# A graph and expert kernel: POOL in the layer norms between two layers, one product for nodes and scores, transposed counts copied by ACT, buffers for the scatters' rows

## The chip, the cores and the metric

The kernel runs on one core of one Trainium2 chip. A core has five engines that work side by side, each through its own list of instructions, in order: TensorE (PE, matrix products, with weight loads PEld beside them), VectorE (DVE), ScalarE (ACT), GpSimd (POOL) and SyncE (SP, which here only starts transfers). Transfers (DMA) are started by SP, ACT or POOL. An instruction that needs another engine's result waits on a semaphore at the head of its engine's list, and all behind it waits too. The metric is the time of one execution in microseconds (us), the median over runs.

## The reference

Four layers on 3125 nodes of 256 features with 50000 edges, each with a residual:

```python
x = x + gnn(layernorm(x))                 # L0_gnn: three graph convolutions
x = x + experts(layernorm(x))             # L0_ffn: 16 experts, best 2, layer norm behind
x = x + attention(layernorm(x))           # L1_gnn: graph attention, 4 heads, 64 wide
x = x + experts(layernorm(x))             # L1_ffn: 8 experts, best 2

def L0_ffn(x):                            # x: [nodes, 256]
    logits = x @ gate_w + gate_b
    top_w  = softmax(top2(logits))
    y = x + sum_k top_w[k] * expert[top_idx[k]](x)      # relu(x @ w1 + b1) @ w2 + b2
    return (y - mean(y)) / sqrt(var(y) + 1e-5) * gamma + beta

def L1_gnn(h):
    x  = h @ W                            # 256 -> 64
    el = x @ Wl.T ; er = x @ Wr.T         # scores, 4 heads each
    ...                                   # softmax over edges, weighted sums, elu
```

A graph convolution sums over edges, which the kernel does as a product with a dense matrix of edge counts between nodes.

## The kernel before

The nodes are padded to 3200, 25 tiles of 128 rows, in seven blocks (`BLK`): four of 512 nodes (4 tiles) and three of 384 (3 tiles). The stages follow each other:

1. 0 to 55 us: edges are loaded and turned into keys (L1194 to L1290).
2. 55 to 295: the counts (L1314 to L1365). For each window of destinations DVE makes one-hot rows `os` (L1323) and `od` (L1326), PE multiplies them into `pc` (L1328), ACT copies the sums to `cr` (L1331). For each of the 25 tiles PE transposes `cr` in four groups (1024, 1024, 1024 and 128 columns, L1337) into `pt`, a copy brings each group to `ct`, PE sums `ct` (`op`, L1344), and SP stores it in DRAM as `cntT`. The copies are ACT's (L1342), but from tile 8 on that of the first group is DVE's (L1340). `pt` and `ct` have two buffers each.
3. 295 to 855: three graph convolutions (L1411 to L1452). A block's sums `agg` (L1431) go to `aT` (the first half copied by DVE, L1434), through the product `gout` (L1440) and `gy` (DVE, L1443) to X. In the third layer each finished block goes on to the norm and to `R0.route` (`Router.steps`, L787 to L910), which picks two experts for each token. For each token it makes a row `meta` of 8 numbers (L858 to L872) and two places `at_i0`, `at_i1` (L903), and POOL scatters the rows to DRAM (`slots`, L905), one indirect DMA for each tile and choice. `meta` and `at_i` come from the pool `gp`, with two buffers. The steps of a block's routing are spread among PE's products for the next blocks.
4. 855 to 883: the last block's routing and the plan of the experts.
5. 883 to 1144: the first expert layer (`experts`, L968 to L1142): ACT copies `cT` (L1090), loads of `w1t` and `slot`, gathers `xs` (L1017, POOL), products (L1038, L1048), results scattered to `res` (L1065, POOL).
6. 1144 to 1237: the end of that layer (L1499 to L1565), the stage that changes most, below.
7. 1237 to 1772: attention (L1572 to L1722), with the second routing inside it, 1772 to 1800 its end and plan.
8. 1800 to 2093: the second expert layer and the output.

Stage 6 runs for each block: for each tile `results` (L1144) loads the two results of each token as `r` (SP, ten buffers), PE adds `r[:,0]`, `r[:,1]` and the base as three products with the identity (L1150, `rsum`), ACT copies the sum to HB (L1151). Then DVE takes the moments (`moments`: L692, L693 and L695, square root by ACT L675, a Newton step by DVE L680 to L685), makes z = (HB - mean) * gamma (L1515) and X += z * rstd (L1517), and the moments of X for the attention's layer norm, with `nm` = -mean * rstd (L1521). ACT makes h (L1525), PE transposes it (L1528), ACT copies `hT` (L1529), PE makes `px`, the projection with nodes along the columns (L1532), ACT copies it to `xT` (L1533). For each tile PE makes the scores `pe` from `xT` (L1536) and, from `hT` once more, the projection with nodes along the rows, `py` (L1539), which ACT copies to `xn` (`spare`, L1541). At the end DVE copies all scores from `pe` to `lr` (L1542), and the first step of the attention takes their maximum (L1545). A scheduler orders every engine's list by priorities; where a pool has no free buffer for a tile, its first instruction waits for the readers of the last one.

Of the kernel before, what the change touches and what calls it, by code (L numbers as in the profile page):

```python
# [8 lines left out]
F32 = mybir.dt.float32  # L9
BF16 = mybir.dt.bfloat16  # L10
F16 = mybir.dt.float16
I32 = mybir.dt.int32
F32R = mybir.dt.float32r
AF = mybir.ActivationFunctionType
OP = mybir.AluOpType
# [4 lines left out]
P = 128  # L20
# [574 lines left out]
def fast(  # L595
# [35 lines left out]
    nc = tc.nc  # L631
    N, D = x.shape
    (NE,) = src.shape
    NT = -(-N // P)
    NP = NT * P
    REAL = N // NT
    DC = D // P
# [15 lines left out]
    small = ctx.enter_context(tc.tile_pool(name="small", bufs=2))  # L653
# [7 lines left out]
    ident = consts.tile([P, P], F32, name="ident")  # L661
# [76 lines left out]
    class Router:  # L738
# [48 lines left out]
        def steps(self, H, t0, U, work, psum, h0=None, pe=lambda i: i, kept=None):  # L787

            h0 = t0 if h0 is None else h0
            E, nm = self.E, self.name  # L790

            def wt(name, shape, dt=F32):
                return work.tile(shape, dt, name=f"{name}_{nm}", tag=f"{name}_{nm}")
# [6 lines left out]
            for n in kept or [4] * (U // 4) + [U % 4] * (U % 4 > 0):  # L800
                hb = work.tile([P, DC, 4 * P], F32, name=f"hb_{nm}", tag=f"hb_{nm}", bufs=1)
                for u in range(n):
                    pt = psum([P, DC, P])
# [48 lines left out]
                                                   op0=OP.mult, op1=OP.add)  # L852
                    cur = rest
            yield
            meta = wt("meta", [P, U, 8])
            if not kept:
                self.keep(H[:, h0:h0 + U, :], t0, U)
            nc.vector.tensor_copy(meta[:, :, 0], tok2[:, t0:t0 + U])  # L858
# [35 lines left out]
            for i in range(2):  # L894
                at = wt(f"at{i}", [P, U])
                nc.vector.tensor_tensor(hots[i], hots[i], row, op=OP.mult)
                nc.vector.tensor_reduce(at, hots[i], axis=AX.X, op=OP.add)
                off = wt(f"off{i}", [P, U])
                nc.vector.tensor_scalar(off, drop[:, t0:t0 + U], float((E * NT + 1) * P + i * PADS), unreal,
                                        op0=OP.add, op1=OP.mult)  # L900
                nc.vector.scalar_tensor_tensor(at, at, real, off, op0=OP.mult, op1=OP.add)
                at_i = wt(f"at_i{i}", [P, U], I32)
                nc.vector.tensor_copy(at_i, at)  # L903
                for u in range(U):
                    d = nc.gpsimd.indirect_dma_start(  # L905
                        out=self.slots, out_offset=bass.IndirectOffsetOnAxis(ap=at_i[:, u:u + 1], axis=0),
                        in_=meta[:, u, :], in_offset=None)
                    for e in self.sent:
                        tc.declare_no_dep(d.ins, e.ins, reason="every token has slots of its own")
                    self.sent.append(d)  # L910
# [230 lines left out]
            with tc.If(rest < E * NT):  # L1141
                tiles(most, TT)  # L1142

        def results(self, base, t, pool, psum):  # L1144

            r = pool.tile([P, 2, D], F32, name="r", bufs=10)
            nc.sync.dma_start(r, self.res[2 * P * t:2 * P * (t + 1), :].rearrange("(p k) d -> p k d", k=2))
            p = psum([P, D])
            for k, v in enumerate((r[:, 0, :], r[:, 1, :], base[:, t, :])):
                nc.tensor.matmul(p, ident, v, start=(k == 0), stop=(k == 2))  # L1150
            nc.scalar.copy(base[:, t, :], p)  # L1151


# [16 lines left out]
    with tc.tile_pool(name="edges", bufs=1) as ed, tc.tile_pool(name="ework", bufs=2) as ew:  # L1170
# [134 lines left out]
        with tc.tile_pool(name="ps_cnt0", bufs=2, space=PSUM) as ps_cnt0, \  # L1305
# [6 lines left out]
            for b, (s0, bw) in enumerate(BLK):  # L1312
                cr = ew.tile([P, NT, bw], F16, name="cr", tag="cr")
                nc.gpsimd.memset(cr.rearrange("p t (u q) -> p t u q", q=P)[:, :, :, REAL:], 0.0)  # L1314
                for dt in range(s0 // P, (s0 + bw) // P):
                    o = dt * P - s0
                    while wins and wins[0][0] < (dt + 1) * REAL:
                        i, w, c = wins.pop(0)
                        pc = ps_cnt0.tile([P, 512], F32, name="pc")
                        for k in range(c):  # L1320
                            if j % OS == 0:
                                os_ = ew.tile([P, P, OS], F16, name="os", bufs=3)
                                nc.vector.tensor_tensor(os_, ramps, by[0][:, None, j:j + OS].to_broadcast([P, P, OS]),  # L1323
                                                        op=OP.is_equal)
                            od = ew.tile([P, 512], F16, name="od", bufs=6)
                            nc.vector.tensor_scalar(od[:, :w * NT], ramp[:, :w * NT], by[1][:, j:j + 1], None,  # L1326
                                                    op0=OP.is_equal)
                            nc.tensor.matmul(pc[:, :w * NT], os_[:, :, j % OS], od[:, :w * NT], start=(k == 0), stop=(k == c - 1))  # L1328
                            j += 1
                        u = o + i - dt * REAL  # L1330
                        nc.scalar.copy(cr[:, :, u:u + w], pc[:, :w * NT].rearrange("p (d t) -> p t d", t=NT))  # L1331
                    ct = ew.tile([P, NP], F16, name="ct")
                    for q0 in range(0, NP, 1024):
                        w2 = min(1024, NP - q0)
                        pt = ps_tr.tile([P, 1024], F16, name="pt")
                        for q in range(w2 // P):
                            nc.tensor.transpose(pt[:, q * P:(q + 1) * P], cr[:, q0 // P + q, o:o + P], ident16)  # L1337

                        if dt >= 8 and q0 == 0:
                            nc.vector.tensor_copy(ct[:, q0:q0 + w2], pt[:, :w2])  # L1340
                        else:
                            nc.scalar.copy(ct[:, q0:q0 + w2], pt[:, :w2])  # L1342
                    for b2, (q0, w2) in enumerate(BLK):
                        nc.tensor.matmul(op[b2 // 4][32 * (b2 % 4):32 * (b2 % 4) + 32, :w2], ones16,  # L1344
                                         ct[:, q0:q0 + w2], start=(dt == 0), stop=(dt == NT - 1))
                        nc.sync.dma_start(cntT[b2][:, dt, :], ct[:, q0:q0 + w2])
                    if dt == 1:
                        R0.clear(HB[:, 9 * R1.Q:])
                        R1.clear(HB[:, :9 * R1.Q])
                    if dt == 8:  # L1350
                        mv, r = moments(X)
                nc.sync.dma_start(cnt[b], cr)
                ip = ps_in.tile([P, 512], F32, name="ip")
                for t in range(NT):
                    q = 32 * (t % 4)
                    nc.tensor.matmul(ip[q:q + 32, :bw], ones16, cr[:, t, :], start=(t < 4), stop=(t >= NT - 4))
                nc.scalar.copy(ins[:, s0:s0 + bw], ip[:, :bw])
                for t in range(s0 // P, (s0 + bw) // P):
                    nc.tensor.matmul(dg[:, 1, t:t + 1], ins[:, t * P:(t + 1) * P], c32, start=True, stop=True)
# [112 lines left out]
    xT = g1.tile([OD, NP], F32, name="xT")  # L1472
    spare = g1.tile([P, NH, 512], F32, name="spare")
    xn = spare.rearrange("p h n -> p (h n)")[:, :NT * OD].rearrange("p (t o) -> p t o", o=OD)
    lr = g1.tile([P, NT, 2, NH], F32, name="lr")
    fa = g1.tile([P, NT, NH], F32, name="fa")
    pj = g1.tile([P, NT, NH], F32, name="pj")
    wj = g1.tile([P, NT, NH], F32, name="wj")
# [3 lines left out]
    with tc.tile_pool(name="moe0", bufs=1) as mp:  # L1482
# [16 lines left out]
        with tc.tile_pool(name="ps_pre", bufs=2, space=PSUM) as ps, tc.tile_pool(name="tail", bufs=1) as mp:  # L1499
# [4 lines left out]
            nc.tensor.transpose(pw, wlr, ident[:2 * NH, :2 * NH])  # L1504
            nc.vector.tensor_copy(wlrT, pw)
            nc.vector.tensor_copy(wlb, wlrT[:, 0:NH, None].to_broadcast([OD, NH, P]))
            pe = ps.tile([P, NT, 2 * NH], F32, name="pe", bufs=1)
            for s0, w in BLK:
                t0, n = s0 // P, w // P
                for t in range(t0, t0 + n):  # L1510
                    R0.results(HBn, t, mp, rsum)
                mv, r = moments(HBn, t0, n)
                for i in range(n):
                    z = mp.tile([P, D], F32, name="z", bufs=2)
                    nc.vector.scalar_tensor_tensor(z, HBn[:, t0 + i, :], mv[:, i, 0:1], gamma,  # L1515
                                                   op0=OP.subtract, op1=OP.mult)
                    nc.vector.scalar_tensor_tensor(X[:, t0 + i, :], z, r[:, i:i + 1], X[:, t0 + i, :],  # L1517
                                                   op0=OP.mult, op1=OP.add)
                mv, r = moments(X, t0, n)
                nm = small.tile([P, n], F32, name="nm", tag="nm")  # L1520
                nc.vector.scalar_tensor_tensor(nm, mv[:, :, 0], -1.0, r, op0=OP.mult, op1=OP.mult)  # L1521
# [9 lines left out]
                for f in range(DC):  # L1531
                    nc.tensor.matmul(px[:, :w], wg[:, f, :], hT[:, f, :w], start=(f == 0), stop=(f == DC - 1))  # L1532
                nc.scalar.copy(xT[:, s0:s0 + w], px[:, :w])  # L1533
                for i in range(n):
                    t = t0 + i
                    nc.tensor.matmul(pe[:, t, :], xT[:, t * P:(t + 1) * P], wlrT, start=True, stop=True)  # L1536
                    py = ps.tile([P, OD], F32, name="py", tag="py")
                    for f in range(DC):
                        nc.tensor.matmul(py, hT[:, f, i * P:(i + 1) * P], wg[:, f, :],  # L1539
                                         start=(f == 0), stop=(f == DC - 1))  # L1540
                    nc.scalar.copy(xn[:, t, :], py)  # L1541
            nc.vector.tensor_copy(lr.rearrange("p t s h -> p t (s h)"), pe)  # L1542
            a_, b_ = lr[:, :, 0, :], lr[:, :, 1, :]
            top = small.tile([P, NH], F32, name="top")
            nc.vector.tensor_reduce(top, a_.rearrange("p t h -> p h t"), axis=AX.X, op=OP.max)  # L1545
# [228 lines left out]
```

## Time and profile before

Three runs took 2101.62, 2096.23 and 2097.72 us, the median is 2097.72. The profiled execution took 2094.98 us, with a span of 2093.2 us and a mean granted TensorE clock of 0.956. By stage (us busy):

| stretch | length | PE | DVE | ACT | POOL | clock |
|---|---|---|---|---|---|---|
| 0 to 55 edges | 55 | 8.0 | 39.6 | 2.1 | 25.0 | 1.00 |
| 55 to 295 counts | 240 | 213.3 | 210.1 | 159.6 | 6.5 | 1.00 |
| 295 to 660 convolutions 1, 2 | 365 | 355.4 | 88.2 | 215.2 | 0.0 | 0.98 |
| 660 to 883 convolution 3, routing | 223 | 185.4 | 105.0 | 92.5 | 54.2 | 0.90 |
| 883 to 1144 experts 1 | 261 | 250.9 | 99.5 | 71.4 | 113.2 | 0.96 |
| 1144 to 1237 end of experts 1 | 93 | 79.3 | 57.4 | 43.6 | 0.1 | 0.89 |
| 1237 to 1800 attention | 563 | 532.1 | 495.2 | 129.5 | 64.7 | 0.95 |
| 1800 to 2093 experts 2 | 293 | 269.0 | 93.2 | 77.8 | 105.5 | 0.94 |

An engine that is busy for most of a stretch may set its length; where none is, the stretch is a chain of waits between them, and the waits of that stretch have to be read.

### The profile page before, as it was taken

Reading aid. Unit: us, or ns where it says so; the run is one execution under the profiler, and the core shown is the slowest. Engines: PE = TensorE matmul, PEld = TensorE weight load, DVE = VectorE, ACT = ScalarE, POOL = GpSimd, SP = SyncE. Lnnn points to the kernel's source line nnn. Section 1 sums busy time; section 2 is a strip of 40 time slices with the busy share of each in tenths; the row PEclk is TensorE's granted clock in tenths of the full one; section 3 lists DMA queues with packets and bytes.
Section 4 is the critical chain, followed back from the end, with each engine's and each line's share of the span. In section 5 each row is a group of like instructions: output and inputs, shape, how many; then the busy total and the mean of one; then the engine's idle time right before and its main releaser. Section 6 shows DMA issues by size and latency. Waiting matters only on the chain. (4 is left out here: it accounts for less than half of the span.)

```text
span 2093.2 us, 31963 instructions
## 1 busy us (share of the span) xinstructions
PE 1893.4 (90%) x10944; PEld 1252.0 (60%) x10944; DVE 1188.1 (57%) x3825; ACT 791.7 (38%) x1611; POOL 369.1 (18%) x414
## 2 busy tenths in 40 slices
PE   1898979999999898699998988999999998699997
PEld 1444548898898677588887741222223232588886
DVE  7998863131124344443332768899998998434330
ACT  0367766565555534222222561212212222222221
POOL 4000000000000312254443000000300402344430
PEclk9999989999999999789999989999999999599998
DMA  5145664344344333665664601111011110465656
GB/s 148 53 176 217 227 220 133 110 129 129 116 115 147 112 91 94 198 201 168 182 192 139 213 1 51 39 48 61 28 54 43 43 39 28 122 182 164 193 160 197
DMA packets 172299, 259.91 MB, mean 124 GB/s; under 512 B 33476, under 2 KB 116658, under 8 KB 171100
## 3 DMA queue, kind: packets, MB, share of 16 engines
q1 hardware_dynamic: 148446, 211.87, 32.6%
q0 software_dynamic: 16016, 37.00, 5.6%
q10 hardware_dynamic: 7662, 8.84, 1.3%
q8 instruction: 93, 1.52, 0.3%
q14 instruction: 82, 0.67, 0.1%
HBM read 187.38 MB, written 70.27 MB: 123 GB/s over the span
## 5 line engine op out<-in xcount | busy, mean ns | idle before, releaser
L1431 PE MATMUL agg<-ar,parts 128*128 128x512 f32 (+1 forms) x2100 | 447.8, 371 | 7.6 <-ACT parts L1419 7.6
L1431 PEld LDWEIGHTS agg<-ar,parts 128*128 128x128 f32 x2100 | 383.6, 189 | 55.0 <-ACT parts L1419 7.7
L1702 DVE SCALAR_TENSOR_TENSOR HB<-ub,wj,cload 128x512 f32<-128x512 f32 (+1 forms) x420 | 268.6, 689 | 21.2 <-ACT ub L1606 9.9
L1426 ACT CAST ar<-cload 128x2560 fp32r<-128x2560 f16 (+1 forms) x105 | 220.8, 2103 | 147.1 <-PE agg L1431 133.5
L1038 PE MATMUL ph<-xsT,w1t 128*128 128x128 f32 x1792 | 239.2, 285 | 12.2 <-DVE xsT L1028 11.1
L1042 ACT ACTIVATE hid<-ph,b1s 128x128 f32<-128x128 f32 x448 | 128.1, 369 | 322.0 <-PE ph L1038 310.1
L1038 PEld LDWEIGHTS ph<-xsT,w1t 128*128 128x128 f32 x1792 | 220.4, 196 | 47.0 <-DVE xsT L1028 30.5
L1048 PE MATMUL py<-w2all,hid 128*128 x896 | 211.9, 380 | 0.0
L1590 PE MATMUL att<-HB,xp 128*64 128x512 f32 (+1 forms) x840 | 187.5, 567 | 0.0
L1048 PEld LDWEIGHTS py<-w2all,hid 128*128 128x128 f32 x896 | 162.1, 191 | 17.5
L1326 DVE TENSOR_SCALAR od<-ramp,by 128x450 f16<-128x450 f16 (+11 forms) x588 | 152.3, 320 | 22.1 <-PE pc L1328 21.0
L1434 DVE COPY aT<-agg 128x512 f32<-128x512 f32 (+1 forms) x21 | 13.3, 633 | 248.5 <-PE agg L1431 248.5
L1328 PE MATMUL pc<-od,os 128*128 128x450 f16 (+11 forms) x588 | 136.6, 334 | 17.6 <-DVE od L1326 9.5
L1059 DVE TENSOR_TENSOR to_i<-to,two 128x1 int32<-128x1 f32 x112 | 17.7, 158 | 237.4 <-DMA res_m<-y,to_i 237.4
L1065 POOL DMA_INDIRECT res_m<-y,to_i x112 | 110.4, 986 | 232.6 <-DVE y L1064 228.3
L905 POOL DMA_INDIRECT slots_m<-meta_m,at_i_m x100 | 107.8, 1078 | 209.0 <-DVE at_i_m L903 122.2
L1331 ACT CAST cr<-pc 128x400 f16<-128x400 f32 (+10 forms) x202 | 95.5, 503 | 63.8 <-PE pc L1328 48.9
L1017 POOL DMA_INDIRECT xs<-feats_m,slot x112 | 108.3, 967 | 61.7 <-issue 23.8
L1590 PEld LDWEIGHTS att<-HB,xp 128*64 128x64 f32 x840 | 51.8, 137 | 107.7 <-issue 61.1
L1328 PEld LDWEIGHTS <-os 128*128 128x128 f16 x588 | 62.2, 118 | 77.9 <-DVE od L1326 20.6
L1590 PE MATMUL sums<-HB,pj 128*32 128x512 f32 (+1 forms) x840 | 102.6, 561 | 0.0
L1440 PE MATMUL gout<-g0w,aT 128*128 128x256 f32 x300 | 78.3, 417 | 20.5 <-DVE aT L1434 15.7
(332 smaller groups left out, 2350.0 us busy)
## 6 DMA issues: line engine op xcount, KB each, us to landing
cload<-cnt SPq DMA_DIRECT2D x60, 640.0 KB
w1t<-in_L_ffn_w_dram SPq DMA_DIRECT2D x56, 512.0 KB
w1t<-in_L_ffn_W_dram SPq DMA_DIRECT2D x52, 512.0 KB
cload<-cnt SPq DMA_DIRECT2D x45, 480.0 KB
cntT<-ct SPq DMA_DIRECT2D x100, 128.0 KB
cnt<-cr SPq DMA_DIRECT2D x4, 3200.0 KB
cload<-cntT SPq DMA_DIRECT2D x20, 640.0 KB
r<-res_m SPq DMA_DIRECT2D x50, 256.0 KB
```

Source lines behind the costliest of these rows:

```text
L905: d = nc.gpsimd.indirect_dma_start(out=self.slots, out_offset=bass.IndirectOffsetOnAxis(ap=at_i[:, u:u + 1], axis=0), in_=meta[:, u, :], i ...
L1017: nc.gpsimd.indirect_dma_start(out=xs, out_offset=None, in_=self.feats, in_offset=bass.IndirectOffsetOnAxis(ap=slot[:, 5:6].bitcast(I32), ...
L1038: behind(nc.tensor.matmul(ph[:, c, :], w1t[:, f, c * P:(c + 1) * P], xsT[:, f, :], start=(f == 0), stop=(f == DC - 1)), "PE")
L1042: nc.scalar.activation(hid[:, c, :], ph[:, c, :], func, bias=self.b1s[:, c, j:j + 1])
L1048: behind(nc.tensor.matmul(py, hid[:, c, :], w2all[:, bass.ds(r, 1), c, :].rearrange("p o d -> p (o d)"), start=(c == 0), stop=(c == FC - 1 ...
L1065: d = nc.gpsimd.indirect_dma_start(out=self.res, out_offset=bass.IndirectOffsetOnAxis(ap=to_i, axis=0), in_=y, in_offset=None)
L1326: nc.vector.tensor_scalar(od[:, :w * NT], ramp[:, :w * NT], by[1][:, j:j + 1], None, op0=OP.is_equal)
L1328: nc.tensor.matmul(pc[:, :w * NT], os_[:, :, j % OS], od[:, :w * NT], start=(k == 0), stop=(k == c - 1))
L1426: nc.scalar.copy(ar[:, :, :w], a[:, :, :w])
L1431: nc.tensor.matmul(agg[f][:, :w], parts[:, t, i, f * P:(f + 1) * P], ar[:, k, :w], start=(t == 0 and i == 0), stop=(t == NT - 1 and i == 1))
L1590: return chain(nc.tensor.matmul(*args, **kw))
L1702: nc.vector.scalar_tensor_tensor(e[:, h, :w], ub[:, h, :w], wj[:, t, h:h + 1], a[:, k, :w], op0=OP.max, op1=OP.mult)
```

## The change

In the scatters' steps, `meta` and the places come from the pool `plans` with four buffers, one size for all blocks and both routers. In the counts all copies of transposed groups are ACT's. At the end of the first expert layer, POOL adds the two results of a token before PE adds the base; ACT makes z = HB * rstd - mean * rstd, POOL multiplies it by gamma, DVE adds it to X; and the scores and the projection along the rows come from one product of `xT` with a matrix `turn` that holds the identity (64 columns) and the scores' weights (8 columns), for a whole block in one PSUM tile, copied by two instructions of ACT. `lr` moves from the pool `gat1` to `tail`.

```diff
-            meta = wt("meta", [P, U, 8])
+            meta = plans.tile([P, 8, 8], F32, name="meta", bufs=4)[:, :U, :]
...
-                at_i = wt(f"at_i{i}", [P, U], I32)
+                at_i = plans.tile([P, 8], I32, name=f"at_i{i}", bufs=4)[:, :U]
...
-        def results(self, base, t, pool, psum):
+        def results(self, base, t, pool, psum, beside=False):
             r = pool.tile([P, 2, D], F32, name="r", bufs=10)
             nc.sync.dma_start(r, self.res[2 * P * t:2 * P * (t + 1), :].rearrange("(p k) d -> p k d", k=2))
             p = psum([P, D])
-            for k, v in enumerate((r[:, 0, :], r[:, 1, :], base[:, t, :])):
-                nc.tensor.matmul(p, ident, v, start=(k == 0), stop=(k == 2))
+            terms = [r[:, 0, :], r[:, 1, :], base[:, t, :]]
+            if beside:
+                two = pool.tile([P, D], F32, name="two_r", bufs=3)
+                nc.gpsimd.tensor_tensor(two, r[:, 0, :], r[:, 1, :], op=OP.add)
+                terms[:2] = [two]
+            for k, v in enumerate(terms):
+                nc.tensor.matmul(p, ident, v, start=(k == 0), stop=(k == len(terms) - 1))
             nc.scalar.copy(base[:, t, :], p)
...
-                        if dt >= 8 and q0 == 0:
-                            nc.vector.tensor_copy(ct[:, q0:q0 + w2], pt[:, :w2])
-                        else:
-                            nc.scalar.copy(ct[:, q0:q0 + w2], pt[:, :w2])
+                        nc.scalar.copy(ct[:, q0:q0 + w2], pt[:, :w2])
...
-            pe = ps.tile([P, NT, 2 * NH], F32, name="pe", bufs=1)
+            turn = mp.tile([OD, OD + 2 * NH], F32, name="turn")
+            nc.vector.tensor_copy(turn[:, :OD], ident[:OD, :OD])
+            nc.vector.tensor_copy(turn[:, OD:], wlrT)
+            lr = mp.tile([P, NT, 2, NH], F32, name="lr")
...
-                    R0.results(HBn, t, mp, rsum)
+                    R0.results(HBn, t, mp, rsum, True)
                 mv, r = moments(HBn, t0, n)
+                nm = small.tile([P, n], F32, name="nm", tag="nm")
+                nc.vector.scalar_tensor_tensor(nm, mv[:, :, 0], -1.0, r, op0=OP.mult, op1=OP.mult)
                 for i in range(n):
-                    z = mp.tile([P, D], F32, name="z", bufs=2)
-                    nc.vector.scalar_tensor_tensor(z, HBn[:, t0 + i, :], mv[:, i, 0:1], gamma,
-                                                   op0=OP.subtract, op1=OP.mult)
-                    nc.vector.scalar_tensor_tensor(X[:, t0 + i, :], z, r[:, i:i + 1], X[:, t0 + i, :],
-                                                   op0=OP.mult, op1=OP.add)
+                    z = mp.tile([P, D], F32, name="z", bufs=3)
+                    nc.scalar.activation(z, HBn[:, t0 + i, :], AF.Identity, bias=nm[:, i:i + 1], scale=r[:, i:i + 1])
+                    nc.gpsimd.tensor_tensor(z, z, gamma, op=OP.mult)
+                    nc.vector.tensor_tensor(X[:, t0 + i, :], z, X[:, t0 + i, :], op=OP.add)
...
                 nc.scalar.copy(xT[:, s0:s0 + w], px[:, :w])
+                py = ps.tile([P, 4, OD + 2 * NH], F32, name="py", tag="py")
                 for i in range(n):
-                    t = t0 + i
-                    nc.tensor.matmul(pe[:, t, :], xT[:, t * P:(t + 1) * P], wlrT, start=True, stop=True)
-                    py = ps.tile([P, OD], F32, name="py", tag="py")
-                    for f in range(DC):
-                        nc.tensor.matmul(py, hT[:, f, i * P:(i + 1) * P], wg[:, f, :],
-                                         start=(f == 0), stop=(f == DC - 1))
-                    nc.scalar.copy(xn[:, t, :], py)
-            nc.vector.tensor_copy(lr.rearrange("p t s h -> p t (s h)"), pe)
+                    nc.tensor.matmul(py[:, i, :], xT[:, (t0 + i) * P:(t0 + i + 1) * P], turn, start=True, stop=True)
+                nc.scalar.copy(xn[:, t0:t0 + n, :], py[:, :n, :OD])
+                nc.scalar.copy(lr.rearrange("p t s h -> p t (s h)")[:, t0:t0 + n, :], py[:, :n, OD:])
```

More of the change, by code (lines that the diff above doesn't have):

```diff
@@ L1474, in fast @@
     xn = spare.rearrange("p h n -> p (h n)")[:, :NT * OD].rearrange("p (t o) -> p t o", o=OD)
-    lr = g1.tile([P, NT, 2, NH], F32, name="lr")
     fa = g1.tile([P, NT, NH], F32, name="fa")
```

## The prediction, before the run

> **What bounds the kernel now.** I read the page's slices first, then window sums, waits and timelines of the four stretches that the change touches.
>
> ```profile
> PE   1898979999999898699998988999999998699997
> DVE  7998863131124344443332768899998998434330
> ACT  0367766565555534222222561212212222222221
> PEclk9999989999999999789999989999999999599998
> ```
> A slice is 52.3 us. TensorE is nearly full nearly everywhere; its dips are slices 15 to 17 (GCN layer 3 with the routing) and 22 (the tail of the first expert layer).
>
> ```profile
> 171.00:292.00 121.00, 107.01 (x909) 61.29 (x910) 98.46 (x362) 94.45 (x187) 1.44 (x4) 1.00 0.57 207
> 1144.00:1237.00 93.00, 79.28 (x386) 57.78 (x386) 57.36 (x264) 43.58 (x127) 0.07 (x1) 0.89 0.39 132
> ```
> Columns after the length: PE, PEld, DVE, ACT and POOL busy, clock, DMA share, GB/s. In the second half of the counts (171 to 292) PE, DVE and ACT are all above 78%: none has much room. In the tail no engine is full; POOL does nothing.
>
> ```profile
> ACT cr L1331 <- PE pc L1328: 10.0, 40, 0.7
> ACT ct L1342 <- PE pt L1337: 7.3, 11, 0.9
> ACT ct L1342 <- DMA cntT<-ct: 4.4, 5, 1.3
> PEld L1328 <- DVE od L1326: 5.0, 17, 0.3
> ```
> Waits of 171 to 292: total, times, longest. ACT's idle time there is in short pieces behind TensorE.
>
> ```profile
> 1188.73 1.58 ACT L1525 ACTIVATE h<-X,nm,rstd 128x256 f32<-128x256 f32 x3 [0.35 <-DVE nm L1521]
> 1191.49 0.22 ACT L1541 COPY spare<-py 128x64 f32<-128x64 f32 x1
> 1197.27 1.57 ACT L1525 ACTIVATE h<-X,nm,rstd 128x256 f32<-128x256 f32 x3
> ```
> ```profile
> 1189.41 0.88 DVE L1517 SCALAR_TENSOR_TENSOR X<-z,rstd,X 128x256 f32<-128x256 f32 x2
> 1194.03 0.16 DVE L695 TENSOR_SCALAR ve<-mv 128x4 f32<-128x4 f32 x1
> 1196.13 0.16 DVE L1521 SCALAR_TENSOR_TENSOR nm<-mv,rstd 128x4 f32<-128x4 f32 x1
> ```
> One cycle of the tail: while ACT makes h of block 2 and copies its transposes, DVE by itself already makes z, X and the second norm of block 3. The two engines overlap; a cycle takes 1197.27 - 1188.73 = 8.54 us. By the same timeline the seven blocks' first h start at 1169.15, 1177.8, 1188.7, 1197.3, 1205.5, 1213.0 and 1223.0: 53.85 us for six cycles.
>
> ```profile
> DVE meta_m L858 <- DMA slots_m<-meta_m,at_i_m: 48.1, 5, 11.8
> 848.86 0.17 DVE L903 CAST at_i_m<-at_m 128x3 int32<-128x3 f32 x1
> 853.96 0.56 DVE L1434 COPY aT<-agg 128x384 f32<-128x384 f32 x1 [4.92 <-PE agg L1431]
> 855.34 0.97 POOL L905 DMA_INDIRECT slots_m<-meta_m,at_i_m  x1 [0.30 <-issue]
> ```
> In layer 3 (660 to 860) DVE stands five times at L858 until the scatters just issued have landed. The last graph block, though, meets no such wait: its aT copy starts when its sums are done.
>
> **The change, part by part.** The sum is made against the profiled execution, 2094.98 us, 2.74 below the median of 2097.72; I add the difference to the median.
>
> *Scatters' own rows, four buffers.* In the changed kernel's instruction order L858 of the first four blocks is hoisted to the kernel's start; block b+4 needs block b's buffer, and its L858 stands on DVE after L903 of block b, where L858 of block b+2 stood before, waiting for the same scatters. The five stalls therefore stay, and a sixth comes: L858 of a later block now waits for block 5's six scatters right ahead of the last block's aT. The last of them is issued at 855.34 and ends at 856.31. In the first of the five stalls the last scatter's row ended at 696.33, L858 started at 697.78 and aT at 698.08: 1.45 and 0.30 later. So L858 starts at 857.76 and aT at 858.1 in place of 853.96: **+4.1** us. Behind aT wait gout, the moments, the route, its scatters and the experts, all one chain. Bounds 0 (if other buffers came free) to +5. The hoisted rows are 12 small DVE operations of 0.09 to 0.18 between L1259's; those outside DVE's 3.76 us wait at 20.8 lie on its chain: **+0.8** (0 to +1.5).
> At both expert starts cT (L1090) and the first w1t fetches waited for the last scatter, because their memory lay over the rows (ACT idle 14.66 before cT at 882.71; slot loads behind both at 885.28). Now only the slot loads wait: 885.28 - 882.71 = 2.57 saved in the first layer, 1802.92 - 1800.56 = 2.36 in the second, of which I take 2 since the products of L1099 still wait there: **-4.5** together (0 to -5).
>
> *Transposed counts by ACT.* 17 copies of 128x1024 leave DVE (0.69 each, 11.8) for ACT (1.02 each in the L1342 row, 17.3). ACT would have 94.5 + 17.3 = 111.8 of 121. Its waits at tile ends (7.3 + 4.4 + 2.6 for L1357 + 1.5) must recur, since it works in order: 127.6, or +6.6; TensorE's waits on DVE's copy and sums (0.6 + part of 5.0) give back 1: **+5.5**. If every copy lay on the path it were +17, if the ten us of waits for pc and DVE's relief covered all, -5.
>
> *Tail.* Removed from PE: 25 rsum products (two passes of 0.216: 10.8) and 100 py products; from DVE: 25 x (0.475 + 0.479) less 25 additions at 0.42 (L1448's row, same shape). Added: 25 z on ACT (0.59 as L1525), 50 additions or products of 128x256 on POOL. No row shows POOL at this: DVE's 0.42 is the lower bound, POOL's 128x403 memset (0.84 to 0.90) the upper; I take 0.6, the memset's rate for 256 elements being 0.56.
> The Trainium skill speaks against this part: by its "GPSIMD Engine Reference" (section 3.1) a two-input operation takes GpSimd about 2.6 cycles an element, which is 0.55 us for 256 before its dispatch, about twice DVE; that lies inside my bounds. Its "SBUF — State Buffer" (practical consequences) adds that a DVE instruction with two SBUF inputs and a GpSimd one that reads SBUF block each other, and the new X addition is such; no row here shows it, and 25 such waits of half an operation would make this part some 7 us longer.
> The relief hardly counts, since PE was not what the cycle ended on alone; the order does. ACT's list is now h h h hT hT h hT, then z of the *next* block: the work that DVE did meanwhile starts only then. One cycle from rows: h to z 2.76 (1188.73 to 1191.49, same instructions); z 0.59, POOL 0.6 and three crossings, 1.3; X to the end of ve 4.78 (1189.41 to 1194.19) less two z (0.8) plus POOL's slower pace (0.4), 4.4; ve to the end of nm 2.1 (1194.19 to 1196.29); 0.1 to h: 10.7. Three-tile blocks save 0.8 on ACT and 0.9 on DVE. Three cycles of 10.7, one of 9.8, one of 9.0, and the last, with no further stats, 8.3: 59.2 against 53.85, +5.4. After the last h, L1542 (0.37) and py products go, three ACT copies come: -0.5; On SP's queue the 25 r loads now stand ahead of both w2all loads, which nobody wants before the second layer's first product at some 1816, and POOL in place of PE frees r's ten buffers; the first block gains by that what POOL's addition ahead of its sums costs: 0. If POOL costs 0.9, the pace adds 4 x 0.3 a cycle, +7. Together **+5** (-4 to +16).
>
> Sum: 4.1 + 0.8 - 4.5 + 5.5 + 5 = +10.9; 2094.98 + 10.9 = 2105.9, and 2.74 more at the median: **2109**.
>
> **Rivals.**
> *The tail falls to its busiest engine (faster).* If ACT always had z or h ready, a cycle would be its own work: 4 x (0.5 + 0.27 + 0.5 + 0.28) + xT 0.5 + xn 0.4 + lr 0.2 + two sqrt 0.4 = 7.7, with three tiles 6.1; three, one of 7.3 and two of 6.1 are 42.6, a gain of 11. With the counts hidden under ACT's idle 26 us (0) and the rest as above: -11 + 0.4 = -10.6, 2087. It decides from the point where z runs before h of the block ahead; for it speaks the idle 50 us of ACT, against it the order of the list.
> *Covers hold (no change).* The counts at 0 and the tail at 0: +0.4, 2098. For it: PE's relief of 23 us in a stage where it was 85% busy; against it the same chain.
> *POOL sets the tail.* POOL at 0.9 or blocked by DVE: tail 5 + 7 of pace + 2 for blocking = +14, sum +19.9, 2118. For it: two POOL steps lie in series in each cycle, and r's sum queues in front of z on POOL; against it: 50 x 0.9 is 45 of 93 us.
> *The row buffers do what they seem to.* If the five stalls vanished, PE's waits of 15.7 and 4.8 in 660 to 860 would go: with the rest, 2109 - 20.5 - 4.1 = 2084. Against it: four buffers are taken up from the start.
>
> **How the numbers follow.** Forecast 0.64, POOL sets the tail 0.18, covers hold 0.09, the two faster ones 0.09 together. A measurement of this kernel tells 0.3%, 6.3 us, from no change, so slower begins at 2104.0 and faster ends at 2091.4. The forecast's own range is 2102 to 2116, of which some 0.08 of chance lies under 2104. Slower: 0.56 of the forecast, 0.18, 0.01 of covers: 0.75. Same: 0.08 + 0.08 + 0.01 of the faster ones: 0.17. Faster: 0.08. A range of 8 in 10 takes in covers hold below and most of POOL's above: 2097 to 2122.
>
> **What would show it.** Right: L858 waiting before the last aT, which starts some 4 us after its sums; six routing stalls; ACT over 90% busy in 171 to 292 and the last L1344 some 5 us later; tail cycles of 10 to 11 us with ACT waiting for nm and DVE for POOL's z; cT before the last scatter's landing. Wrong: tail cycles under 9 us, the stage of the counts unchanged, or POOL operations near 1 us.

## The result: slower by 1.3%, more than twice what was forecast

The changed kernel takes 2125.04 us in the median (2122.82 to 2132.26, four runs), the kernel before 2098.7 beside it; the ratio is 1.0134, with a 95% interval of 1.0109 to 1.0160. Forecast were 2109 and a range of 2097 to 2122. The profiled execution took 2127.23 us with a span of 2125.4, 32.2 us above the span before. The medians differ by 26.3: the profiled execution before was faster than all four of the timed ones, so some 6 us of the differences below are scatter between executions.

To see where the 32.2 us lie I cut both profiles at the same instructions. The last column is what the prediction's steps said for that stretch.

| stretch, from to | before | after | difference | forecast |
|---|---|---|---|---|
| start to the first product of the counts | 55.01 | 54.92 | -0.1 | +0.8 |
| counts, to their last `op` | 240.60 | 247.23 | +6.6 | +5.5 |
| to the first aT | 37.32 | 36.84 | -0.5 | 0 |
| first aT to the last of convolution 2 | 305.23 | 310.18 | +5.0 | 0 |
| to the last aT of convolution 3 | 215.80 | 223.84 | +8.0 | +4.1 |
| to the first expert product | 39.94 | 38.15 | -1.8 | -2.6 |
| first expert layer, to its last result scatter | 249.20 | 247.92 | -1.3 | 0 |
| tail, to `nsh` | 90.91 | 105.66 | +14.8 | +5 |
| attention, to its last group of sums on DVE | 530.23 | 530.19 | 0.0 | 0 |
| to the second layer's first product | 48.22 | 43.89 | -4.3 | -2 |
| second expert layer | 233.64 | 238.48 | +4.8 | 0 |
| output | 47.10 | 48.10 | +1.0 | 0 |

Three rows hold most of the miss: convolutions 1 and 2, which no part of the change computes in; the last aT; and the tail. A fourth, the second expert layer, is taken up at the end of the account. The page after, slices of 53.1 us:

```profile
PE   1898879999999988699997778999999998799997
POOL 4000000000000312244443510000300402444430
PEclk9999989999999999789999959999999999699998
```

Counted from 1, slices 22 to 24 hold the tail: PE shows 7 7 7 where 8 9 8 stood, POOL 3 5 1 where 3 0 0 stood, and the clock in slice 24 is 5 in place of 8. The two stages that were changed most, by window (columns as before: length, PE, PEld, DVE, ACT, POOL, clock, DMA share, GB/s):

```profile
171.00:301.00 130.00, 113.51 (x947) 63.78 (x947) 88.72 (x344) 111.69 (x205) 1.49 (x3) 1.00 0.54 199
1162.00:1267.00 105.00, 70.08 (x234) 40.92 (x235) 55.11 (x237) 53.52 (x139) 38.63 (x50) 0.73 0.33 114
```

In the counts ACT is now the fullest engine but PE, 111.69 of 130. In the tail every engine has slack, PE is busy for 9 us less, and yet the stage is longer and the granted clock fell from 0.89 to 0.73. Waits of the counts, same window:

```profile
DVE od L1332 <- PE pc L1334: 34.4, 28, 3.3
ACT cr L1337 <- PE pc L1334: 10.2, 43, 0.7
ACT ct L1344 <- PE pt L1343: 3.2, 8, 0.8
ACT ct L1344 <- DMA cntT<-ct: 1.1, 2, 0.8
PE pc L1334 <- ACT cr L1337: 5.6, 27, 0.4
```

DVE, relieved of 17 copies, waits 34.4 us where it waited 16.2: its free time bought nothing. ACT is at work or waits for a short while, mostly for TensorE, in 128 of the 130 us, and TensorE's products wait for ACT's copies in turn.

The wait ahead of the last aT, in DVE's timeline after:

```profile
860.24 0.17 DVE L904 CAST at_i<-at_m 128x3 int32<-128x3 f32 x1
872.70 0.17 DVE L859 COPY meta<-tok 128x6 f32<-128x6 f32 x1 [12.29 <-DMA slots_m<-meta,at_i]
873.01 0.55 DVE L1436 COPY aT<-agg 128x384 f32<-128x384 f32 x1
```

aT comes 12.77 us after the last `at_i`, where it came 5.10 after it before. The place was forecast, the length was not. And one back-to-back run of products in convolution 1, before and after:

```profile
363.36 22.84 PE L1431 MATMUL agg<-ar,parts 128*128 128x512 f32 x99
```
```profile
369.91 23.36 PE L1433 MATMUL agg<-ar,parts 128*128 128x512 f32 x99
```

99 products without a gap take 22.84 and 23.36 us at a granted clock of 1.00 in both windows: 230.7 and 236.0 ns each. A block of 512 nodes takes 26.8 us in place of 26.3.

### The profile page after: what moved, and what is told of

Same layout as the page of the kernel before. It is cut to its first block, busy times and chain, and to the rows that moved or that the text cites. A ratio compares the mean times of both kernels' runs of the same rounds, so it can differ in the third digit from the quotient of the medians.

```text
span 2125.4 us, 31659 instructions
## 1 busy us (share of the span) xinstructions
PE 1897.1 (89%) x10794; PEld 1240.4 (58%) x10794; DVE 1181.8 (56%) x3791; ACT 819.0 (39%) x1642; POOL 407.2 (19%) x464
## 4 chain that ended last, share of the span: by engine, by line
PE 39%; issue 9%; DMA 5%; DVE 5%; POOL 5%; ACT 2%; SPq 0%; POOLq 0%; ACTq 0%; DVEq 0%
PE att L1592 12%; PE sums L1592 7%; PE ph L1039 5%; PE py L1049 4%; DMA res_m<-y,to_i 3%; PE agg L1433 2%; POOL xs L1018 2%; PE misc L1156 2%; POOL slots_m L906 2%; PE pl L1592 1%; DMA slots_m<-meta,at_i 1%; PE gout L1442 1%; ACT xp L1692 1%; PE misc L812 1%; POOL res_m L1066 1%
## 5 line engine op out<-in xcount | busy, mean ns | idle before, releaser
L1433 PE MATMUL agg<-ar,parts 128*128 128x512 f32 (+1 forms) x2100 | 456.6, 376 | 7.6 <-ACT parts L1421 7.6
L906 POOL DMA_INDIRECT slots_m<-meta,at_i x100 | 108.0, 1080 | 209.1 <-DVE at_i L904 110.1
L1337 ACT CAST cr<-pc 128x400 f16<-128x400 f32 (+10 forms) x202 | 95.3, 503 | 64.8 <-PE pc L1334 49.2
```

What stands on the lines that cost most here:

```text
L906: d = nc.gpsimd.indirect_dma_start(out=self.slots, out_offset=bass.IndirectOffsetOnAxis(ap=at_i[:, u:u + 1], axis=0), in_=meta[:, u, :], i ...
L1433: nc.tensor.matmul(agg[f][:, :w], parts[:, t, i, f * P:(f + 1) * P], ar[:, k, :w], start=(t == 0 and i == 0), stop=(t == NT - 1 and i == 1))
```

## The experiments

Each kernel is compared with the kernel before in runs of its own session; that kernel's median differed between sessions (2112.8, 2110.9 and 2100.5 us), so only ratios and stretches are used. A stretch comes from one profiled execution and is set against the profile before. The tail of the six kernels that leave it as it was (before, e1, e2, e4, e5, e6) took 89.3 to 92.7 us, so a difference of 2 us there says nothing.

**e1_rows4: the row buffers alone.**

```diff
-            meta = wt("meta", [P, U, 8])
+            meta = plans.tile([P, 8, 8], F32, name="meta", bufs=4)[:, :U, :]
-                at_i = wt(f"at_i{i}", [P, U], I32)
+                at_i = plans.tile([P, 8], I32, name=f"at_i{i}", bufs=4)[:, :U]
-    lr = g1.tile([P, NT, 2, NH], F32, name="lr")
+            lr = mp.tile([P, NT, 2, NH], F32, name="lr")
```

> The kernel before with the scatters' rows in four buffers of their own as the only part of the change (lr moves to the pool of the tail to make room). Theory A (the rows' buffers bring both the sixth wait and, by moving the GCN's tiles in memory, its slower products): a block of 512 nodes in the first convolution takes 26.8 us from aT to aT as in the changed kernel, not 26.3; the last aT waits behind the rows, +4; experts start some 2 to 4 us earlier twice; in all +5 to +10 us. Theory B (the slower products belong to the chip's state or to another part): blocks stay at 26.3, and the sum is -2 to +2 us.

Ratio 1.0042 (1.0026 to 1.0058), +9 us. Blocks take 26.81 us, so the slower products come with this part. The last aT waits behind the rows here too; its POOL and SP timelines and the window of the wait show what ran meanwhile:

```profile
859.71 0.97 POOL L905 DMA_INDIRECT slots_m<-meta,at_i  x1 [0.30 <-issue]
```
```profile
858.77 14.28 SPq L964 DMA_DIRECT2D w2all<-in_L_ffn_w_dram  x4
```
```profile
861.00:866.00 5.00, 0.00 (x0) 0.00 (x0) 0.24 (x3) 0.00 (x0) 0.00 (x0) 0.68 1.08 354
```

The last scatter's row ends at 860.68 and L858 starts at 865.73, 5.05 us later, not the 1.45 of the first such wait. From 858.77 on SP fetches the experts' weights, four transfers of 2 MB, at 354 GB/s with the DMA engines full, and PE does nothing for five us. The scatters' small packets land among these. The changed kernel and e12 show the same in this place (5.09 and 5.22 us), while the five earlier waits of every kernel that has them end 1.15 to 1.59 us after the last row. No experiment moved the weights' transfers, so this cause is read from the times alone.

**e2_act: the transposed copies alone.**

```diff
-                        if dt >= 8 and q0 == 0:
-                            nc.vector.tensor_copy(ct[:, q0:q0 + w2], pt[:, :w2])
-                        else:
-                            nc.scalar.copy(ct[:, q0:q0 + w2], pt[:, :w2])
+                        nc.scalar.copy(ct[:, q0:q0 + w2], pt[:, :w2])
```

> The kernel before with ACT making all transposed copies as the only part. Theory: the counts end 6.6 us later, as in the changed kernel, and all behind them moves with it: +6 to +7 us in all. Rival (the 6.6 us come from the row buffers' extra instructions at the start, or from elsewhere): 0 to +2 us. If the GCN's products become slower here too (26.8 us a block), the slower products come from the counts' part.

Ratio 1.0035 (1.0020 to 1.0050), +7 us. The counts take 247.83 us where they took 240.6, the way to the first aT 1.5 less; blocks stay at 26.30. The theory holds.

**e3_tail: the tail alone**, all three of its parts.

```diff
-                    R0.results(HBn, t, mp, rsum)
+                    R0.results(HBn, t, mp, rsum, True)
...
+                    nc.scalar.activation(z, HBn[:, t0 + i, :], AF.Identity, bias=nm[:, i:i + 1], scale=r[:, i:i + 1])
+                    nc.gpsimd.tensor_tensor(z, z, gamma, op=OP.mult)
+                    nc.vector.tensor_tensor(X[:, t0 + i, :], z, X[:, t0 + i, :], op=OP.add)
...
+                    nc.tensor.matmul(py[:, i, :], xT[:, (t0 + i) * P:(t0 + i + 1) * P], turn, start=True, stop=True)
```

> The kernel before with the end of the first expert layer changed as the only part. Theory: from the last scatter of results to nsh it takes 105.7 us as in the changed kernel, not 90.9: +15 us in all, the GCN's blocks at 26.3 us. Rival (the tail was slow for a late start or a lower clock inherited from the stages before): +5 us or less.

Ratio 1.0077 (1.0053 to 1.0102), +16 us; from the last result scatter to `nsh` 106.23 us. The tail's loss is its own and owes nothing to the stages before. Blocks at 26.30. The three parts alone, e1 to e3, add up to 1.54%, the whole change to 1.34% (1.09 to 1.60).

**e4_pad: moving the GCN's tiles without changing anything.**

```diff
+        gp.tile([P, 320], F32, name="pad", bufs=1)
         R0.ready(f0_b1, f0_b2, plans)
```

> The kernel before with an unused tile of 1280 bytes per partition ahead of the GCN's tiles, which moves ar, aT, parts and the count loads up by 1280 bytes and changes nothing else. Theory A1 (the place in memory sets the pace of the GCN's products): a block of 512 takes near 26.8 us in place of 26.3, +8 us in all. Theory A2 (not the place): 26.3 us and 0 us.

Ratio 0.9999 (0.9981 to 1.0017), blocks at 26.31: A1 fell for this move. What e4 did not change is the distance between `ar`, which PE streams, and `parts`, which it loads as weights: in e1 and in the changed kernel the old row buffers, 384 bytes, left the pool between the two, so that `ar` moved by 1280 bytes and `parts` by 896.

**e5_rows7: no row waits at all; e6_rows7_shift: the same with that distance changed.** In e5 the old tiles are kept as dead space, in e6 they are not.

```diff
             meta = wt("meta", [P, U, 8])
+            if self is R0:
+                meta = rows[0].tile([P, 4, 8], F32, name="meta7", bufs=7)[:, :U, :]
...
                 at_i = wt(f"at_i{i}", [P, U], I32)
+                if self is R0:
+                    at_i = rows[0].tile([P, 4], I32, name=f"at7_{i}", bufs=7)[:, :U]
...
         parts = gh.tile([P, NT, 2, D], F32R, name="parts")
+        rows.append(gh)
```

> The kernel before with seven buffers for the rows of the first router, behind parts in the GCN's own pool, so that no row waits in layer 3; ar and parts stay where they were. Theory: the wait of 48 us on DVE is gone; PE's 15.7 and 4.8 us of waiting for aT and gy in 660 to 860 go with it, layer 3 takes 196 to 200 us from aT to aT in place of 216 to 219, blocks stay at 26.3: -15 to -20 us in all. Rival (the stall is hidden by something that ends later, such as the scatters on POOL): -5 us or less.

> As e5_rows7, but without the old buffers being kept in place: parts moves down by 384 bytes per partition, ar stays. In the changed kernel and in e1_rows4 ar moved by 1280 and parts by 896, so parts moved against ar by the same -384; in e4_pad both moved by 1280 and nothing slowed. Theory R (the distance between ar and parts sets the pace of the products): blocks of 512 take 26.8 us here, +8 us against e5_rows7. Rival (something else in the change of the rows slows the products): 26.3 us, as fast as e5_rows7.

e5: ratio 0.9933 (0.9908 to 0.9958), -15 us. Layer 3 takes 188.3 us from aT to aT where e4 took 219.2 and the kernel before 215.8; some 6 us come back ahead of the first expert product (46.0 in place of 39.9), where the slot loads then wait in the same stream of weights. Another 7 come back right behind it: the first result scatter follows 18.6 us after this product, before it was 11.6 (9.2 to 14.8 in the kernels without seven buffers). Some 14 of the 27.5 us are left at that point, near the whole gain. DVE's longest wait of layer 3 in e5 no longer names the rows:

```profile
DVE aT L1440 <- PE agg L1437: 48.3, 6, 19.6
```

e6: ratio 0.9971 (0.9957 to 0.9984), 7.6 us above e5 by the medians, blocks at 26.82. The same run of products in e5 and in e6:

```profile
363.08 23.07 PE L1437 MATMUL agg<-ar,parts 128*128 128x512 f32 x100
```
```profile
364.29 23.58 PE L1439 MATMUL agg<-ar,parts 128*128 128x512 f32 x100
```

Theory R was borne out: with `parts` 384 bytes lower these products take 2.2% longer, in the profiles 7.4 us over the three convolutions. But in all these runs `ar` stood at its old place or 1280 bytes above it, and `parts` at its old place or 1280 above (26.3 us a block), 896 above or 384 below (26.8). The old place and the one 1280 bytes above differ by a whole multiple of 256 bytes, the slow places lie halfway between such multiples. So the address of `parts` alone fits as well as its distance from `ar`, and no run separates the two.

**e7_z_pool and e8_z_dve: z's path alone, with POOL and with DVE for gamma.** The diff is e7's; e8 has `nc.vector` in place of `nc.gpsimd`.

```diff
                 for i in range(n):
-                    z = mp.tile([P, D], F32, name="z", bufs=2)
-                    nc.vector.scalar_tensor_tensor(z, HBn[:, t0 + i, :], mv[:, i, 0:1], gamma, ...)
-                    nc.vector.scalar_tensor_tensor(X[:, t0 + i, :], z, r[:, i:i + 1], X[:, t0 + i, :], ...)
+                    z = mp.tile([P, D], F32, name="z", bufs=3)
+                    nc.scalar.activation(z, HBn[:, t0 + i, :], AF.Identity, bias=nm[:, i:i + 1], scale=r[:, i:i + 1])
+                    nc.gpsimd.tensor_tensor(z, z, gamma, op=OP.mult)
+                    nc.vector.tensor_tensor(X[:, t0 + i, :], z, X[:, t0 + i, :], op=OP.add)
```

> The kernel before with only z's path changed in the tail (ACT makes z, POOL multiplies by gamma, DVE adds). Theory S (the order does it: z of the next block waits behind h on ACT, and POOL's and DVE's operations of 0.8 and 0.66 lie in series): nearly the whole loss of the tail, +12 to +16 us from the last scatter to nsh. Rival (POOL's sum of the two results, ahead of every rsum, makes the tail slow): +3 us or less here.

> As e7_z_pool, but DVE multiplies by gamma in place of POOL. Theory S1 (ACT's order is what costs): the tail stays about as long as in e7_z_pool, within 3 us. Theory S2 (POOL, with the additions of DVE that run at 0.66 in place of 0.42 while POOL works, is what costs): the additions take 0.42 again and the tail is 6 us or more shorter than in e7_z_pool.

e7: ratio 1.0039 (1.0018 to 1.0061), its tail 102.68 us, +11.8. e8: 1.0063 (1.0044 to 1.0081), its tail 101.06, +10.2. With DVE in POOL's place the additions run at 0.417 us again, but the tail is only 1.6 shorter: S1 holds, S2 falls for z alone. From the first block's h to the last one's, e7 takes 64.4 us and e8 65.0, where the kernel before takes 53.85 and the changed kernel 66.1. In the first three of these six cycles, all but one at a granted clock of 1.00 (0.94 in the changed kernel's third), e7 takes 34.2 us, e8 35.7, the changed kernel 33.8 and the kernel before 28.1: the order costs 6 to 8 us there, with POOL or without. The groups of e8, of e7 and of the whole change, mean in ns behind the busy time:

```profile
L1518 DVE TENSOR_TENSOR z<-z,gamma 128x256 f32<-128x256 f32 x25 | 10.2, 420 | 18.4 <-ACT z L1517 18.4
L1519 DVE TENSOR_TENSOR X<-z,X 128x256 f32<-128x256 f32 x25 | 10.0, 417 | 0.2
```
```profile
L1518 POOL TENSOR_TENSOR z<-z,gamma 128x256 f32<-128x256 f32 x25 | 18.5, 756 | 69.4 <-ACT z L1517 49.2 <-PE rsum L1150 19.4 <-DVE X L1519 0.5
L1519 DVE TENSOR_TENSOR X<-z,X 128x256 f32<-128x256 f32 x25 | 14.6, 595 | 23.6 <-POOL z L1518 23.3
```
```profile
L1522 POOL TENSOR_TENSOR z<-z,gamma 128x256 f32<-128x256 f32 x25 | 20.1, 820 | 35.0 <-ACT z L1521 34.7
L1153 POOL TENSOR_TENSOR two_r<-r 128x256 f32<-128x256 f32 x25 | 18.8, 752 | 15.5 <-DMA r<-res_m 8.5 <-PE rsum L1156 5.9
L1523 DVE TENSOR_TENSOR X<-z,X 128x256 f32<-128x256 f32 x25 | 16.2, 660 | 21.5 <-POOL z L1522 21.5
```

In all three the operation that ACT feeds waits longest for ACT's z (18.4, 49.2, 34.7), as the order would have it. Theory S had asked for +12 us or more in e7, 11.8 came.

**e9_one and e10_add: the other two parts of the tail.** First e9, the one product with its two copies, then e10, POOL's sum of the two results.

```diff
-                    nc.tensor.matmul(pe[:, t, :], xT[:, t * P:(t + 1) * P], wlrT, start=True, stop=True)
-                    for f in range(DC):
-                        nc.tensor.matmul(py, hT[:, f, i * P:(i + 1) * P], wg[:, f, :], ...)
-                    nc.scalar.copy(xn[:, t, :], py)
+                    nc.tensor.matmul(py[:, i, :], xT[:, (t0 + i) * P:(t0 + i + 1) * P], turn, start=True, stop=True)
+                nc.scalar.copy(xn[:, t0:t0 + n, :], py[:, :n, :OD])
+                nc.scalar.copy(lr.rearrange("p t s h -> p t (s h)")[:, t0:t0 + n, :], py[:, :n, OD:])
```
```diff
+                two = pool.tile([P, D], F32, name="two_r", bufs=3)
+                nc.gpsimd.tensor_tensor(two, r[:, 0, :], r[:, 1, :], op=OP.add)
+                terms[:2] = [two]
```

> The kernel before with only the one product for nodes and scores (turn), its two copies and lr in the tail's pool. Theory: PE loses 100 products, ACT 18 copies, nothing new waits, and since the tail's cycle is shared by PE, ACT and DVE the stage shortens by 3 to 8 us. Rival (xT now stands between px and py, a longer chain): 0 or longer by up to 3.

> The kernel before with only POOL's addition of the two results. Theory: POOL's 0.7 us stands ahead of the first rsum, PE loses 10.8 us in a stage where it waits anyway: the tail changes by -3 to +2 us. Rival (POOL's reading of two operands slows DVE's X by the shared path): DVE's operations with two SBUF operands become longer than 0.48 and the tail is +3 or more.

e9: ratio 0.9952 (0.9934 to 0.9971), tail 87.10, -3.8: a gain. The medians differ by 9.4 us; its profiled execution was the slowest of ten, and where the other 5 or 6 us lie is not shown. e10: the tail is 91.97, +1.1, as its theory said; its ratio is 0.9967 (0.9947 to 0.9987) all the same. In its profile the second expert layer takes 227.6 us in place of 233.6 with the same list of instructions; what the part alone is worth to the whole stays open. The rival was half right: DVE's z with HB and gamma became longer, 582 ns in place of 475, X 535 in place of 479, but the stage absorbed it:

```profile
L1520 DVE SCALAR_TENSOR_TENSOR z<-HB,mv,gamma 128x256 f32<-128x256 f32 x25 | 14.2, 582 | 0.1
```

**e11_rows7_one: the two parts that gain, together** (the diffs of e5 and e9).

> e5_rows7 with the one product of e9_one, the parts of the change that should gain. If both gains stand alone, the sum of those of e5_rows7 (-15) and of e9_one: -18 to -23 us, near 2090 where the kernel before takes 2111. If the tail's gain is lost to the clock or to its chain: as e5_rows7.

Ratio 0.9888 (0.9853 to 0.9923), 2077.30 against 2100.48: -23 us, near the sum of both (-15 and -9). Its tail takes 83.44 us. The ratio puts it under the kernel before, and so under the changed kernel.

**e12_after_gap: the changed kernel with the old distance.**

```diff
+        gh.tile([P, 96], F32, name="gap")
         parts = gh.tile([P, NT, 2, D], F32R, name="parts")
```

> The changed kernel with 384 unused bytes ahead of parts, so that ar and parts stand as far from each other as before the change. Theory R: blocks of 512 back at 26.3 us, and some 8 us of the changed kernel's loss gone, all else as in the changed kernel: +18 to +22 us against the kernel before in place of +26 to +30. Rival: blocks at 26.8.

Blocks are back at 26.31 and the way from the first aT to the end of convolution 2 at 305.3. The ratio, 1.0119 (1.0080 to 1.0158), cannot be told from that of the changed kernel: in layer 3 the gain is not seen (225.7 against 223.8). There the first five steps from aT to aT agree with those of the changed kernel within 0.1 us although the products are faster: the stalls behind the scatters set the pace. So in the changed kernel the place of `parts` is shown to cost 5 us, not the 8 that were expected of it.

## Why the prediction was wrong

The direction was forecast, the size was not: +10.9 was summed, about +27 came. The steps that failed are the tail, mis-sized by 10 us, the wait ahead of the last aT, mis-sized by some 2 to 4, and the pace of the convolutions' products, put at nothing and worth 5. By the steps:

- *Tail*: +5 was summed, +14.8 came. The order that the prediction named, z of the next block behind h on ACT, is a cause (e7 and e8: 10 to 12 us with it alone), but its price was too low, and one term was left at nothing. The six cycles took 66.1 us where 59.2 were summed: the first three 33.8 (32.1 summed), the last three 32.3 (27.1 summed). The cycle that the prediction took apart is the second, after the change on ACT, DVE and POOL:

```profile
1199.46 1.58 ACT L1530 ACTIVATE h<-X,nm,rstd 128x256 f32<-128x256 f32 x3 [0.73 <-DVE rs_r L680]
1202.27 0.60 ACT L1521 ACTIVATE z<-HB,nm,rstd 128x256 f32<-128x256 f32 x1
1210.84 1.58 ACT L1530 ACTIVATE h<-X,nm,rstd 128x256 f32<-128x256 f32 x3 [0.32 <-DVE rs_r L680]
```
```profile
1203.71 0.42 DVE L1523 TENSOR_TENSOR X<-z,X 128x256 f32<-128x256 f32 x1 [2.70 <-POOL z L1522]
1204.76 0.94 DVE L1523 TENSOR_TENSOR X<-z,X 128x256 f32<-128x256 f32 x1 [0.15 <-POOL z L1522]
1208.86 0.15 DVE L695 TENSOR_SCALAR ve<-mv 128x4 f32<-128x4 f32 x1
```

  h to z is 2.81 (2.76 was summed), z to X 1.44 (1.3), X to the end of ve 5.30 (4.4), from there to nm's end 1.74 (2.1), and 0.1 to h: 11.4 in place of 10.7. Its largest error is X to ve: the first addition takes 0.42, the second, under POOL's products, 0.94. POOL takes 0.82 an operation (its row under e8) in place of 0.6. But this cycle holds only 0.7 of the miss. The dearest is the fourth, 12.44 where 9.8 were summed:

```profile
1221.55:1233.99 12.44, 8.22 (x20) 3.69 (x20) 6.03 (x30) 6.19 (x17) 2.42 (x3) 0.50 0.00 0
1225.76 3.68 PE L1537 MATMUL px<-hT,wg 128*64 128x512 f32 x4 [0.46 <-ACT hT L1534]
1229.48 0.58 ACT L1538 COPY xT<-px 64x512 f32<-64x512 f32 x1 [2.78 <-PE px L1537]
1232.13 0.37 ACT L1543 COPY spare<-py 128x256 f32<-128x256 f32 x1 [2.07 <-PE py L1542]
1232.47 0.22 ACT L675 ACTIVATE rs_s<-ve 128x3 f32<-128x3 f32 x1
```

  Here the granted clock is 0.50 (first line), and px takes 3.68 us; in the second cycle, at a clock of 1.00, the same four products took 1.93. ACT waits 2.78 us for px and 2.07 for py, and the square root of the next norm stands behind these copies in ACT's list: ve ended at 1230.29, the root began at 1232.47. The clock was 0.50, 0.65 and 0.53 in the last three cycles and 1.00 in all six before the change. The prediction had taken TensorE's products out of the chain and had no term for its clock. How much of the 5.2 us of the last three cycles is the clock and how much the order is not separated. In e8, where PE keeps all its products, the clock falls too (0.56 and 0.50 in the last two cycles), in e9, which lacks z's part, in the last one alone (0.53).

  The first block's h came 28.6 us after the last result scatter in place of 26.1, where 0 had been taken. In e10, with POOL's sum alone, it came after 29.15, and the kernels without it took 24.6 to 28.0: the sum ahead of the first block is not made up for. The rival of a dear POOL named the size, tail +14, but not the cause: e8, in which POOL does none of this work, already takes 65.0 us for the six cycles. That its number fits is in good part luck.
- *The wait ahead of the last aT* came where it was forecast, and the five others stayed. The term of 4.1 was mis-sized: it took the landing time of 1.45 us from the first stall, where the DMA engines were under half busy. Here the weights' transfers had begun, and landing took 5.09. The wait put aT 7.7 us later against its `at_i`, and the last step from aT to aT took 30.6 us in place of 24.5. SP's timeline of the profile before has the same four transfers from 854.34 on, with the last aT, so this could have been read. A seventh wait for scatters, of 6.1 us at 904, was not forecast; its stretch came out 1.8 us shorter all the same.
- *Nothing was said of where tiles lie.* That the products of the convolutions could slow with the same instructions was no term of the sum. e4, e5, e6 and e12 show that it follows the place of `parts`; 5 us of the profile's difference, 7 to 8 between e5 and e6.
- *The rows hoisted to the start*: +0.8 was forecast, -0.1 came.
- *The experts' starts*: -1.8 and -4.3 against -2.6 and -2, in sum -6.1 against -4.6.
- *Counts*: +5.5 forecast, +6.6 - 0.5 measured, and 7.2 - 1.5 in e2. The sum was right, its parts were not: ACT's waits at tile ends, which "must recur" with 15.8 us, fell to 5.9 (3.2 + 1.1 + 1.6), and the 10.0 us of waits for pc, which the sum had filled, stayed at 10.2. So ACT did use part of its short waits, and ACT was 86% busy in 171 to 292, not over 90%. That the two errors nearly cancel is luck.
- *Not explained*: the second expert layer's +4.8. Its instruction lists are the same in both kernels, and over the twelve experiments its stretch took 227.6 to 239.1 us, so I put no cause to it.
- *A reading of the page*: the tail was put in slice 22, but 1144 to 1237 lies in slices 22 to 24; nothing in the sum rests on it.

The prediction weighed two rules of the Trainium skill. From "GPSIMD Engine Reference" (section 3.1) it had worked out an estimate of 0.55 us before dispatch; measured are 0.75 to 0.82. And "SBUF — State Buffer" (practical consequences), on blocking between a DVE instruction with two SBUF operands and a GpSimd one that reads SBUF, agrees with the runs: X's addition takes 0.417 with POOL at rest (e8) and 0.595 to 0.660 beside it, while the moments of X, with one operand, stay at 0.41 to 0.42.

## What to carry to other kernels

Before work moves to an engine with slack, follow one cycle through the lists: an engine in order does the new work only where its list has it, and two stages that overlapped may become one chain. Work taken from TensorE is not free time when its clock falls in the gaps: read the granted clock by cycle, and not only over the stage. More buffers help only if there are enough of them that the reuse falls behind the last hot user; four for the rows of eleven blocks added a wait in a worse place, seven for the first router's seven blocks took some 28 us out of layer 3, of which 15 were left in the whole time. And a buffer that moves between pools moves the tiles behind it: look at the pace of unchanged products after the change, before the cause is sought in the code.

## What the runs showed of the hardware that was not expected

- The place in memory of the tile that PE loads as weights set the pace of the GCN's fp32r products: 26.31 us a block with `parts` at its old place or 1280 bytes above it (before, e5; e4, e12), 26.81 with it 896 above or 384 below (e1, after; e6), at a granted clock of 1.00 in the runs of products compared. Only these four places were tried; whether the distance from `ar` or the address of `parts` itself counts is open.
- An indirect scatter of 128 rows of 32 bytes landed 1.15 to 1.59 us after its row's end where the weights' transfers had not begun, and 5.04 to 5.22 us after it while they ran (354 GB/s in e1).
- The granted clock over the tail went from 0.89 to 0.73 as PE's busy time fell from 79.3 of 93 to 70.1 of 105 us, its px products of four tiles from 605 to 722 ns. By cycle it fell to 0.50 behind the third, in which PE was busy for 5.35 of 10.71 us: what was taken from PE was in part given back.
